# Two-sided decayed sums as a backward scan and a forward scan of it, in place, with clamps and one product on GpSimd

## The chip, the cores and the metric

The kernel runs on one core of a Trainium2 chip. A core has TensorE (PE, with its weight loads shown apart as PEld), VectorE (DVE), ScalarE (ACT), GpSimd (POOL) and SyncE (SP), and 16 DMA engines. The time is the device time of one launch in microseconds. Before the change it was 1601.48 us, the median of three runs (1598.72 to 1601.71).

## The reference, cut to what matters

Two layers, each a gated mixture of experts added to x. The gate comes from a conditioning signal that is computed from k = v = fside (4 batches, 512 steps, 512 channels) by a two-sided decayed sum over time. Here x is (4, 512, 512), everything is 32-bit floating point:

```python
def wkv(r, k, v, w, u, time_emb):            # r = x, k = v = fside
    tf    = sigmoid(sum(time_emb, -1))
    decay = exp(-exp(w)) * (0.5 + 0.5 * tf)  # one number for a batch and a channel
    ek, ekv = exp(min(k, 30)), exp(min(k, 30)) * v
    # a_t = decay * a_(t-1) + value_t, forward in time (nf, df) and backward (nb, db)
    euk = exp(min(u + k, 30))
    num = nf + nb - ekv + euk * v
    den = df + db - ek + euk
    return sigmoid(r) * (num / max(den, 1e-8)) * (0.8 + 0.2 * tf)

x = x + ffn0(wkv(x, fside, fside, w0, u0, cond), ...)   # rmsnorm, 8 routed experts, top 2, one shared
x = x + ffn1(wkv(x, fside, fside, w1, u1, cond), ...)   # 32 routed experts, top 6, capacity 512, shared
```

So num and den hold, for each step t, the sum over all steps s of decay^|t-s| times a value (ekv or ek), with one more term for t itself. Only the factor sigmoid(r) differs from layer to layer through x; the rest of layer 1's conditioning depends on fside alone.

## The kernel before

**The unit loop (layer 0's conditioning, L641 to L691).** Channels lie on the 128 partitions and time runs along the row. The work is cut into 16 units n = (b, c): batch b of 4, and one of four blocks of 128 channels; a unit is a tile of 128 x 512. The Python loop writes the order of the instructions on ACT, PE and DVE by hand (`tc.manual_schedule`, L193); POOL and SP are left to a planner, which places an instruction by the costs and the order that it assumes. In one pass of the loop stand, for different units:

- `turn(n + 3)`: PE transposes a block of k's rows (`kr`, one buffer, loaded by SP for a whole batch, L122) and ACT copies it to `kA` (L394, L395). After the last block of a batch the next batch's rows are asked for (L397), into the same buffer.
- `front(n + 1)`, `front_exps(n + 1)`: DVE clamps k and u + k at 30 (L406, L408), ACT takes both exponents (L414).
- `mid(n)`: DVE forms ekv and eukv (L425, L426) and runs four scans (`scans`, L263, L264): for den and for num a forward one, and a backward one of 511 columns that leaves the step itself out. Each writes a tile of its own.
- `sums(n - 1)`: PE adds the forward scan, the backward scan and the last term in PSUM, three pairs of matmuls for den and three for num (L436 to L438; the matrix for num carries the factor -(0.8 + 0.2 tf)). ACT then makes 1/den by logarithm and exponent (L440 to L442).
- `back(n - 1)`: DVE refines the reciprocal, multiplies by num and by sigmoid(x), four operations (L449 to L452). den has two banks of PSUM, num one.

Between these stand layer 0's routing for the batch before (`route_max`, `route_top`, `route_pay`, `route_slots`: some 45 small DVE instructions a batch, and eight indirect writes by POOL into a table in DRAM, L353) and the shared expert of a few token tiles. For batches 0 to 2 each table write waits for the one before it. Before the loop POOL writes the empty tables and fills the DRAM tensor `xb` with zeros, 16 writes of 256 KB (L245 to L254).

**The exponents of layer 1.** From unit 12 on, and in the shared expert's stretch after the loop, `exps1_upto` lets ACT take layer 1's exponents of units 0 to 9 into memory that has come free (`spare`); those of units 10 to 15 follow in `wkv1_rest`.

**Layer 0's routed experts and layer 1's conditioning (L904 to L954).** `routed(0, ...)` goes through 8 experts in tiles of 128 tokens: POOL gathers rows (L772), PE multiplies, ACT evicts, POOL forms `hrow` (L846) and scatters the result (L818). Here POOL, PE and ACT are in the written order and DVE is not: DVE's instructions are placed by the planner. DVE's work in this stretch is `wkv1(n)` for 16 units: clamp (L915), ekv (L916), the four scans, two adds of forward and backward (L918, L919), the terms of the step itself (L920 to L922), a floor (L923), a reciprocal (L924), and the product that replaces k in `kA` (L925). Its tiles are in the pool `rp`. After the last expert come the shared expert's last three token tiles (13, 14, 15; `LATE` is 13): `share_up` on PE (L580), `share_silu` on ACT (L585), `share_hid` on DVE (L591), then `share_turn` and `share_down`.

**The join (L957 to L987).** For each of 16 token tiles, the late ones first, SP loads the two halves of layer 0's result (`acc` from `xa`, L965, and `other` from `xb`, L967; the tiles of `other` are taken where the pool `rp` was), DVE adds them (L968, and L970 for the late tiles), PE transposes, ACT takes the sigmoid, and DVE multiplies by `kA` (L976) to make layer 1's input. Layer 1's shared and routed experts follow and take the rest of the time.

Of the kernel before, what the change touches and what calls it, by code (L numbers as in the profile page):

```python
# [9 lines left out]
F32 = mybir.dt.float32  # L10
# [3 lines left out]
ALU = mybir.AluOpType  # L14
# [11 lines left out]
DEN_MIN = 1e-8  # L26
EXP_LN = "natural_log_exp_and_others"
# [3 lines left out]
def adaln_ffn_kernel(  # L31
# [90 lines left out]
    def load_k(b):  # L122
        kr = wk.tile([P, TB, D], F32, tag="kr", name=f"kr{b}", bufs=1)
        nc.sync.dma_start(kr, kf[b * S : (b + 1) * S, :].rearrange("(i p) c -> p i c", p=P))
        return kr
# [54 lines left out]
    kr = wk.tile([P, TB, D], F32, tag="kr", name="kr0", bufs=1)  # L180
    for i in range(TB):
        nc.scalar.dma_start(kr[:, i, :], kf[i * P : (i + 1) * P, :])
    load_x(0)
    gaten = acc[:E1, NT - 3, :]
# [9 lines left out]
            engines={mybir.EngineType.Activation, mybir.EngineType.PE, mybir.EngineType.DVE}  # L194
# [20 lines left out]
    for l in range(2):  # L215
        ew = const.tile([P, NC], F32, name=f"ew{l}")
        nc.scalar.activation(ew, wch[l], AF.Exp)
        dw = const.tile([P, NC], F32, name=f"dw{l}")
        nc.scalar.activation(dw, ew, AF.Exp, scale=-1.0)
        dec = const.tile([P, NC, B], F32, name=f"dec{l}")  # L220
        nc.vector.tensor_tensor(
            dec, dw.unsqueeze(2).to_broadcast([P, NC, B]), half.unsqueeze(1).to_broadcast([P, NC, B]), ALU.mult
        )
        decay.append(dec)
# [20 lines left out]
    for tb, width in ((table0, 3), (table1, 2)):  # L245
        blank = wk.tile([P, NCOL * width], F32, name=f"blank{width}", tag="lgT", bufs=1)
        bv = blank.rearrange("p (c w) -> p c w", w=width)
        nc.gpsimd.memset(bv, 0.0)
        nc.gpsimd.memset(bv[:, :, 0], EMPTY)
        nc.gpsimd.dma_start(tb.rearrange("(p c) w -> p (c w)", p=P), blank)  # L250
    zero = wk.tile([P, D], F32, name="zero", tag="zr", bufs=TB)
    nc.gpsimd.memset(zero, 0.0)
    for t in range(NT):
        nc.gpsimd.dma_start(xb[t * P : (t + 1) * P, :], zero)  # L254


    L = S - 1

    def scans(l, b, c, ek, ekv, df, dx, nf, nx):

        dec = decay[l][:, c, b : b + 1]
        for v, f, r in ((ek, df, dx), (ekv, nf, nx)):
            nc.vector.tensor_tensor_scan(f, dec.to_broadcast([P, S]), v, 0.0, ALU.mult, ALU.add)  # L263
            nc.vector.tensor_tensor_scan(  # L264
                r[:, L - 1 :: -1],
                v[:, L:0:-1],
                dec.to_broadcast([P, L]),
                0.0,
                ALU.add,
                ALU.mult,  # L270
            )

# [113 lines left out]
    def turn(n):  # L386

        nonlocal kr
        if n >= NU:
            return  # L390
        b, c = units[n]
        pk = bank("tr", f"pk{n}")
        for i in range(TB):
            nc.tensor.transpose(pk[:, i * P : (i + 1) * P], kr[:, i, c * P : (c + 1) * P], ident)  # L394
        nc.scalar.copy(kA[:, c, b * S : (b + 1) * S], pk)  # L395
        if c == NC - 1 and b + 1 < NB:
            kr = load_k(b + 1)  # L397
            load_x(b + 1)

    def front(n):  # L400
        if n >= NU:
            return
        b, c = units[n]
        kT = kA[:, c, b * S : (b + 1) * S]
        ek = wk.tile([P, S], F32, tag="ek", name=f"ek{n}", bufs=2)
        nc.vector.tensor_scalar(ek, kT, 30.0, None, ALU.min)  # L406
        euk = wk.tile([P, S], F32, tag="euk", name=f"euk{n}", bufs=3)
        nc.vector.tensor_scalar(euk, kT, uch[0][:, c : c + 1], 30.0, ALU.add, ALU.min)  # L408
        fronts[n] = ek, euk

    def front_exps(n):
        if n < NU:
            for v in fronts[n]:
                nc.scalar.activation(v, v, AF.Exp)  # L414

    def mid(n):
        b, c = units[n]
        kT = kA[:, c, b * S : (b + 1) * S]
        ek, euk = fronts.pop(n)

        def tmp(tag, bufs=2):
            return wk.tile([P, S], F32, tag=tag, name=f"{tag}{n}", bufs=bufs)

        ekv, eukv = tmp("ekv", 1), tmp("eukv")
        nc.vector.tensor_tensor(ekv, ek, kT, ALU.mult)  # L425
        nc.vector.tensor_tensor(eukv, euk, kT, ALU.mult)  # L426
        df, dx, nf, nx = tmp("df"), tmp("dx"), tmp("nf"), tmp("nx")
        scans(0, b, c, ek, ekv, df, dx, nf, nx)
        mids[n] = (df, dx, euk), (nf, nx, eukv)

    def sums(n):

        b, c = units[n]
        den, num = bank("den", f"den{n}"), bank("num", f"num{n}")
        for p, m, (f, r, o) in zip((den, num), (ident, nfac[:, b, :]), mids.pop(n)):
            nc.tensor.matmul(p, m, f, start=True, stop=False)  # L436
            nc.tensor.matmul(p[:, :L], m, r[:, :L], start=False, stop=False)
            nc.tensor.matmul(p, m, o, start=False, stop=True)  # L438
        r = wk.tile([P, S], F32, tag="r", name=f"r{n}")
        nc.scalar.activation(r, den, AF.Relu, bias=neg_min)  # L440
        nc.scalar.activation(r, r, AF.Ln, bias=pos_min)
        nc.scalar.activation(r, r, AF.Exp, scale=-1.0)  # L442
        mids[n] = den, num, r
# [118 lines left out]
    def route_slots(b):  # L562
# [4 lines left out]
        through(fill_table(table0, sloti, pay, TB, 2, "table0" if b == NB - 1 else None))  # L567
# [53 lines left out]
    def exps1_upto(m):  # L621
        nonlocal done
        while done < m:
# [3 lines left out]
            nc.scalar.activation(ek, kT, AF.Exp)  # L627
# [13 lines left out]
    for n in range(NU + 1):  # L641
        b, c = divmod(n, NC)
        if n:
            sums(n - 1)
        front(n + 1)
# [29 lines left out]
        if c == 3 and b >= 1:  # L675
            route_slots(b - 1)
        if c == 2 and b >= 1:
            route_max(b - 1)
# [33 lines left out]
    route_slots(NB - 1)  # L712
    counts0 = const.tile([P, E0], I32, name="counts0")
# [190 lines left out]
    with tc.tile_pool(name="r0", bufs=1) as rp, tc.tile_pool(name="px0", bufs=1, space=PSUM) as px:  # L904
# [5 lines left out]
        def wkv1(n):  # L910
# [3 lines left out]
            ekv, df, dx, nf, nx = [rp.tile([P, S], F32, tag=f"v{i}", name=f"v{i}_{n}") for i in range(5)]  # L914
            nc.vector.tensor_scalar(ek, ek, E30, None, ALU.min)  # L915
            nc.vector.tensor_tensor(ekv, ek, kT, ALU.mult)  # L916
            scans(1, b, c, ek, ekv, df, dx, nf, nx)
            nc.vector.tensor_tensor(df[:, :L], df[:, :L], dx[:, :L], ALU.add)  # L918
            nc.vector.tensor_tensor(nf[:, :L], nf[:, :L], nx[:, :L], ALU.add)  # L919
            nc.vector.scalar_tensor_tensor(df, euk, E30, df, ALU.min, ALU.add)  # L920
            nc.vector.scalar_tensor_tensor(ekv, euk, E30, kT, ALU.min, ALU.mult)
            nc.vector.tensor_tensor(nf, nf, ekv, ALU.add)  # L922
            nc.vector.tensor_scalar(df, df, DEN_MIN, None, ALU.max)  # L923
            nc.vector.reciprocal(df, df)  # L924
            nc.vector.scalar_tensor_tensor(kT, nf, fac[:, b : b + 1], df, ALU.mult, ALU.mult)  # L925
# [188 lines left out]
```

## Time and profile before

| stretch of the span, us | what runs | PE busy | DVE busy | ACT busy | POOL busy |
|---|---|---|---|---|---|
| 60 to 120 | unit loop | 50.8 | 55.9 | 36.6 | 8.5 |
| 120 to 180 | unit loop with routing | 55.4 | 51.6 | 34.1 | 11.5 |
| 213 to 262 | shared expert, table, first gather | 45.4 | 18.6 | 22.7 | 14.7 |
| 262 to 395 | routed experts 0, `wkv1` on DVE | 112.9 | 133.0 | 61.0 | 89.9 |
| 395 to 468 | the same | 56.4 | 73.0 | 26.7 | 45.5 |
| 468 to 562 | routed experts 0 | 75.0 | 0.0 | 33.4 | 38.5 |
| 580 to 625 | join | 37.4 | 22.5 | 19.0 | 0.0 |

The profiled execution took 1601.9 us, its span (first to last instruction) is 1600.1 us at a mean granted PE clock of 0.963. Over the span PE is busy for 91%, DVE for 42%, POOL for 37% and ACT for 25%. Busy times are sums of instructions in the stretch; POOL's include the issue of its DMAs. In the listings a row gives its start, its duration, the engine, the line and the operation, and in brackets how long the engine had been idle before it and what ended that. Instructions of one engine overlap a little, so the distance from one start to the next is shorter than a duration.

### The profile page before, as it was taken

To read this page: it belongs to the slowest core of one execution; us is meant where nothing else is said; L and a number is where in the kernel's file an instruction comes from. 1 tells how busy PE (TensorE), PEld (TensorE's weight loads), DVE (VectorE), ACT (ScalarE), POOL (GpSimd) and SP (SyncE) were. 2 spreads that over 40 slices of the span, in tenths; PEclk is the share of its full clock that TensorE was granted. 3 is DMA by queue.
4 is the path that set the end of the run, shared out by engine and by line. 5 is a ranking of instruction groups with operands and counts; after the bars stand their busy time and mean duration, and the time that the engine had idled before them with its cause. 6 is when DMAs were issued, how large, how long until landed. Compare 5 with 4: busy or idle time off the path is not lost. (4 is left out here: it accounts for less than half of the span.)

```text
span 1600.1 us, 16354 instructions
## 1 busy us (share of the span) xinstructions
PE 1458.0 (91%) x5097; PEld 860.8 (54%) x5097; DVE 678.1 (42%) x1192; ACT 399.9 (25%) x966; POOL 593.0 (37%) x576
## 2 busy tenths in 40 slices
PE   4878988979788788999999999999999999999997
PEld 2445555656555466444444565555555555655654
DVE  6897956999960035261111222222222222222221
ACT  4755534454333324000000111111111111111110
POOL 3020133767654300016663333344333443433332
PEclk8999999999989879999999999999999999999999
DMA  9210114444545364001113655565645585565542
GB/s 351 80 33 34 40 47 163 73 100 77 111 109 125 86 223 153 1 1 43 39 46 109 181 150 130 145 191 153 164 109 136 128 266 119 130 187 131 122 99 40
DMA packets 117177, 184.95 MB, mean 116 GB/s; under 512 B 19928, under 2 KB 65004, under 8 KB 117016
## 3 DMA queue, kind: packets, MB, share of 16 engines
q1 hardware_dynamic: 80120, 122.14, 22.6%
q0 software_dynamic: 36336, 60.04, 19.8%
q8 instruction: 66, 1.08, 0.3%
q10 hardware_dynamic: 576, 1.05, 0.2%
q14 instruction: 79, 0.65, 0.1%
HBM read 152.07 MB, written 52.64 MB: 128 GB/s over the span
## 5 line engine op out<-in xcount | busy, mean ns | idle before, releaser
L813 PE MATMUL pout<-w,hT 128*128 128x512 f32 (+1 forms) x432 | 206.9, 612 | 10.6 <-ACT hT L804 9.3
L818 POOL DMA_INDIRECT out_dram<-ob,put x52 | 82.6, 1589 | 282.7 <-DVE ob L817 142.2
L772 POOL DMA_INDIRECT acc<-z1d,put x119 | 123.3, 1036 | 136.7 <-PE pza L785 58.9
L353 POOL DMA_INDIRECT table<-pay,r1sloti x96 | 93.3, 972 | 195.1 <-DVE hid L1063 168.6
L851 DVE SCALAR_TENSOR_TENSOR hrow<-pup,tab,sgt 128x352 f32<-128x352 f32 x84 | 49.1, 584 | 257.6 <-issue 131.2
L835 PE MATMUL pgate<-w,zgT 128*128 128x352 f32 x416 | 133.2, 463 | 0.1
L839 PE MATMUL pup<-w,zgT 128*128 128x352 f32 x416 | 131.5, 459 | 0.0
L817 DVE COPY ob<-pout 128x512 f32<-128x512 f32 x84 | 58.1, 692 | 172.7 <-PE pout L813 166.8
L813 PEld LDWEIGHTS pout<-w,hT 128*128 128x128 f32 (+1 forms) x432 | 77.8, 194 | 83.8 <-issue 55.7
L785 PE MATMUL pza<-ident,acc 128*128 128x128 f32 x584 | 88.8, 277 | 21.3 <-DMA acc<-z0d,put 18.1
L785 PEld LDWEIGHTS pza<-ident,acc 128*128 128x128 f32 x584 | 71.7, 142 | 65.3 <-issue 27.5
L353 POOL DMA_INDIRECT table<-r0pay,r0sloti x32 | 36.0, 1125 | 182.9 <-DVE r0sloti L343 137.4
L839 PEld LDWEIGHTS pup<-w,zgT 128*128 128x128 f32 x416 | 79.0, 190 | 44.0
L835 PEld LDWEIGHTS pgate<-w,zgT 128*128 128x128 f32 x416 | 75.8, 192 | 34.0 <-issue 1.2
L808 ACT COPY hT<-phT 96x128 f32<-96x128 f32 x84 | 22.0, 262 | 285.3 <-DVE hT L806 285.3
L1060 PE MATMUL g<-zT,w 128*128 128x512 f32 (+1 forms) x192 | 89.3, 609 | 4.2 <-DVE lg L991 4.2
L795 ACT COPY zgT<-pza 128x256 f32<-128x256 f32 x103 | 38.3, 373 | 210.3 <-DVE zgT L794 158.7
L813 PE MATMUL pout<-zT,hT 128*128 128x512 f32 (+1 forms) x192 | 87.8, 593 | 0.0
L1060 PE MATMUL u<-zT,w 128*128 128x512 f32 (+1 forms) x192 | 86.3, 592 | 0.0
L1069 PE MATMUL o<-w,hid 128*128 128x512 f32 (+1 forms) x192 | 83.8, 592 | 0.0
L835 PE MATMUL pgate<-zT,zgT 128*128 128x352 f32 x256 | 81.0, 459 | 0.0
L839 PE MATMUL pup<-zT,zgT 128*128 128x352 f32 x256 | 81.0, 459 | 0.0
(279 smaller groups left out, 2346.9 us busy)
## 6 DMA issues: line engine op xcount, KB each, us to landing
w<-in_L_ffn_w_dram SPq DMA_DIRECT2D x44, 704.0 KB, 5.9
zT<-in_L_ffn_w_dram SPq DMA_DIRECT2D x20, 704.0 KB, 5.0
w<-in_L_ffn_w_dram SPq DMA_DIRECT2D x22, 512.0 KB
zT<-in_L_ffn_w_dram SPq DMA_DIRECT2D x10, 512.0 KB
w<-in_L_ffn_w_dram SPq DMA_DIRECT2D x22, 192.0 KB, 8.9
xb<-zero POOLq DMA_DIRECT2D x16, 256.0 KB, 7.8
acc<-in_x_dram SPq DMA_DIRECT2D x4, 1024.0 KB, 15.2
z0d<-zr SPq DMA_DIRECT2D x16, 256.0 KB, 2.0
```

The lines of the kernel that those rows point to most:

```text
L353: ins = nc.gpsimd.indirect_dma_start(out=table, out_offset=bass.IndirectOffsetOnAxis(ap=sloti[:, t, j : j + 1], axis=0), in_=pay[:, t, j, ...
L772: nc.gpsimd.indirect_dma_start(out=rows(e, s), out_offset=None, in_=zd, in_offset=bass.IndirectOffsetOnAxis(ap=put_at[:, e * NS + s : e * ...
L785: nc.tensor.transpose(pza[which][:, c * P : (c + 1) * P], rows(e, s)[:, c * P : (c + 1) * P], ident)
L795: nc.scalar.copy(dst[:, h:, :], pza[which][:, h * P :].rearrange("p (c t) -> p c t", c=h))
L813: nc.tensor.matmul(po, hT[:m, j, :], dv[:m, j, :], start=(j == 0), stop=(j == nf - 1))
L817: nc.vector.tensor_copy(row, po)
L818: nc.gpsimd.indirect_dma_start(out=outs[n % len(outs)], out_offset=bass.IndirectOffsetOnAxis(ap=at, axis=0), in_=row, in_offset=None, boun ...
L835: nc.tensor.matmul(pg, zt[:, c, :], gv[:, c, :], start=(c == 0), stop=(c == NC - 1))
L839: nc.tensor.matmul(pu, zt[:, c, :], uv[:, c, :], start=(c == 0), stop=(c == NC - 1))
L851: nc.vector.scalar_tensor_tensor(hrow, pu, tab[:, col, 1:2], sgt, ALU.mult, ALU.mult)
L1060: nc.tensor.matmul(p[:m], wv[:, c, f : f + m], zT[:, c, cols], start=(c == 0), stop=(c == NC - 1))
L1069: nc.tensor.matmul(po, hid[:m, j, i * P : (i + 1) * P], dv[:m, j, :], start=(j == 0), stop=(j == len(FCH) - 1))
```

## The change

A backward scan over all 512 steps, followed by a forward scan of its result, gives at each step the two-sided sum divided by 1 - decay^2, up to the first step, where the backward result has to be multiplied by 1/(1 - decay^2) before the forward scan starts. So `scans` now works in place on one tile of two halves (den's and num's values): two backward scans, one scaling of the first column of both halves, two forward scans. The factor 1 - decay^2 enters as a bias (its logarithm) of the exponent in layer 0, and of layer 1's exponent too, whose clamp is now at 30's exponent times that factor (`cap`). For this each layer gets six more small DVE instructions and one ACT logarithm at the start.

In layer 0 the sums on PE fall from three pairs of matmuls to two each for den and num. The two clamps and the product eukv move from DVE to POOL. POOL joins the engines in the written order; its zero writes to `xb` are spread over the loop (one a pass), the empty tables are written in the pass n = 2, and the table writes of batches 0 to 2 are spread over three passes and no longer wait for each other. k's rows have two buffers, and the rows of batch 1 are asked for at the start, ahead of the gate's and the first experts' weights.

In layer 1 `wkv1` loses the two adds, keeps its clamp (now into the tile `v2`, no longer in place) and the rest.

```diff
-        kr = wk.tile([P, TB, D], F32, tag="kr", name=f"kr{b}", bufs=1)
+        kr = wk.tile([P, TB, D], F32, tag="kr", name=f"kr{b}")
...
     load_x(0)
+    krs.append(load_k(1))
...
-            engines={mybir.EngineType.Activation, mybir.EngineType.PE, mybir.EngineType.DVE}
+            engines={
+                mybir.EngineType.Activation, mybir.EngineType.PE, mybir.EngineType.DVE, mybir.EngineType.Pool
+            }
...
-        decay.append(dec)
+        nc.vector.tensor_scalar(dec, dec, NEAR_1, None, ALU.min)
+        om = const.tile([P, NC, B], F32, name=f"om{l}")
+        nc.vector.tensor_scalar(om, dec, -1.0, 1.0, ALU.mult, ALU.add)
+        nc.vector.scalar_tensor_tensor(om, dec, 1.0, om, ALU.add, ALU.mult)
+        lom = const.tile([P, NC, B], F32, name=f"lom{l}")
+        nc.scalar.activation(lom, om, AF.Ln)
+        inv = const.tile([P, NC, B], F32, name=f"inv{l}")
+        nc.vector.reciprocal(inv, om)
+        cap = const.tile([P, NC, B], F32, name=f"cap{l}")
+        nc.vector.tensor_scalar(cap, om, E30, None, ALU.mult)
+        decay.append((dec, cap, lom, inv))
...
-    def scans(l, b, c, ek, ekv, df, dx, nf, nx):
-
-        dec = decay[l][:, c, b : b + 1]
-        for v, f, r in ((ek, df, dx), (ekv, nf, nx)):
-            nc.vector.tensor_tensor_scan(f, dec.to_broadcast([P, S]), v, 0.0, ALU.mult, ALU.add)
+    def scans(l, b, c, v):
+
+        dec, _, _, inv = (m[:, c, b : b + 1] for m in decay[l])
+        for h in range(2):
             nc.vector.tensor_tensor_scan(
-                r[:, L - 1 :: -1],
-                v[:, L:0:-1],
-                dec.to_broadcast([P, L]),
-                0.0,
-                ALU.add,
-                ALU.mult,
+                v[:, h, ::-1], dec.to_broadcast([P, S]), v[:, h, ::-1], 0.0, ALU.mult, ALU.add
             )
+        nc.vector.tensor_scalar(v[:, :, 0], v[:, :, 0], inv, None, ALU.mult)
+        for h in range(2):
+            nc.vector.tensor_tensor_scan(v[:, h, :], dec.to_broadcast([P, S]), v[:, h, :], 0.0, ALU.mult, ALU.add)
...
-        nc.vector.tensor_scalar(ek, kT, 30.0, None, ALU.min)
+        v = wk.tile([P, 2, S], F32, tag="v2", name=f"v2_{n}", bufs=3)
+        nc.gpsimd.tensor_scalar(v[:, 0, :], kT, 30.0, None, ALU.min)
...
-        nc.vector.tensor_scalar(euk, kT, uch[0][:, c : c + 1], 30.0, ALU.add, ALU.min)
+        nc.gpsimd.tensor_scalar(euk, kT, uch[0][:, c : c + 1], 30.0, ALU.add, ALU.min)
...
-        nc.vector.tensor_tensor(ekv, ek, kT, ALU.mult)
-        nc.vector.tensor_tensor(eukv, euk, kT, ALU.mult)
+        nc.gpsimd.tensor_tensor(eukv, euk, kT, ALU.mult)
+        nc.vector.tensor_tensor(v[:, 1, :], v[:, 0, :], kT, ALU.mult)
+        scans(0, b, c, v)
...
-        for p, m, (f, r, o) in zip((den, num), (ident, nfac[:, b, :]), mids.pop(n)):
-            nc.tensor.matmul(p, m, f, start=True, stop=False)
-            nc.tensor.matmul(p[:, :L], m, r[:, :L], start=False, stop=False)
+        for p, m, (d, o) in zip((den, num), (ident, nfac[:, b, :]), mids.pop(n)):
+            nc.tensor.matmul(p, m, d, start=True, stop=False)
             nc.tensor.matmul(p, m, o, start=False, stop=True)
...
-        through(fill_table(table0, sloti, pay, TB, 2, "table0" if b == NB - 1 else None))
+        writes[b] = fill_table(table0, sloti, pay, TB, 2, "table0")
...
             sums(n - 1)
+            nc.gpsimd.dma_start(xb[(n - 1) * P : n * P, :], zero)
+        if n == 2:
+            blank_tables()
...
             route_slots(b - 1)
+            write_slots(b - 1, 3)
+        if c < 2 and b >= 2:
+            write_slots(b - 2, 3 - c if b < NB else 5)
...
-            ekv, df, dx, nf, nx = [rp.tile([P, S], F32, tag=f"v{i}", name=f"v{i}_{n}") for i in range(5)]
-            nc.vector.tensor_scalar(ek, ek, E30, None, ALU.min)
-            nc.vector.tensor_tensor(ekv, ek, kT, ALU.mult)
-            scans(1, b, c, ek, ekv, df, dx, nf, nx)
-            nc.vector.tensor_tensor(df[:, :L], df[:, :L], dx[:, :L], ALU.add)
-            nc.vector.tensor_tensor(nf[:, :L], nf[:, :L], nx[:, :L], ALU.add)
+            v = rp.tile([P, 2, S], F32, tag="v2", name=f"v2_{n}", bufs=1)
+            cap = decay[1][1][:, c, b : b + 1]
+            nc.vector.tensor_scalar(v[:, 0, :], ek, cap, None, ALU.min)
+            nc.vector.tensor_tensor(v[:, 1, :], v[:, 0, :], kT, ALU.mult)
+            scans(1, b, c, v)
+            d, s = v[:, 0, :], v[:, 1, :]
...
```

## The prediction

> **What bounds the kernel now.** I read the table of stages first (busy microseconds of each engine in stretches that I chose), then the waits, then the VectorE (DVE) timeline around the places that the diff touches. The page's own chain of waits covers 2% of the span and carries nothing. Columns: PE, PEld, DVE, ACT and POOL busy, then the granted clock and the DMA.
>
> ```profile
> 120.00:180.00 60.00, 55.42 (x193) 31.05 (x192) 51.55 (x113) 34.14 (x62) 11.50 (x10) 0.94 0.14 50
> ...
> 213.00:262.00 49.00, 45.40 (x184) 31.07 (x183) 18.56 (x72) 22.70 (x45) 14.73 (x16) 0.97 0.19 65
> 262.00:395.00 133.00, 112.93 (x465) 79.34 (x465) 132.99 (x137) 60.96 (x178) 89.88 (x56) 0.95 0.48 108
> 395.00:468.00 73.00, 56.42 (x223) 38.77 (x221) 73.00 (x77) 26.70 (x87) 45.45 (x32) 0.92 0.47 109
> 468.00:562.00 94.00, 75.04 (x273) 51.54 (x274) 0.00 (x1) 33.40 (x105) 38.49 (x34) 0.86 0.45 103
> ```
>
> Layer 0's unit loop (to 213) is DVE's: one unit follows the next at 9.24 us (46.35 to 55.59) and its DVE instructions fill that. From 213 to 262 PE runs the shared expert. From 262 to 557 PE runs the routed experts of layer 0, while DVE works through layer 1's conditioning (`wkv1`), done at 468. DVE's next work is the last three token tiles of the shared expert and then the join of the layers:
>
> ```profile
> 464.66 3.34 DVE L924 RECIPROCAL v<-v 128x512 f32<-128x512 f32 x1
> 562.54 0.48 DVE L591 SCALAR_TENSOR_TENSOR shr<-pza,rs,ssg 128x256 f32<-128x256 f32 x1 [94.54 <-ACT ssg L585]
> 562.95 0.74 DVE L925 SCALAR_TENSOR_TENSOR kA<-v,fac,v 128x512 f32<-128x512 f32 x1
> 566.00 0.48 DVE L591 SCALAR_TENSOR_TENSOR shr<-pza,rs,ssg 128x256 f32<-128x256 f32 x1 [2.31 <-ACT ssg L585]
> 572.26 0.48 DVE L591 SCALAR_TENSOR_TENSOR shr<-pza,rs,ssg 128x256 f32<-128x256 f32 x1 [5.78 <-ACT ssg L585]
> 580.38 0.69 DVE L968 TENSOR_TENSOR acc<-acc,other 128x512 f32<-128x512 f32 x1 [7.64 <-DMA other<-xb]
> ```
>
> The reader is to see the 94.54 us wait: DVE stands at the first L591 until PE has left the routed experts. It costs nothing, because only one instruction of `wkv1` (L925 of unit 15) is queued behind it before the join.
>
> **Part 1, the order on DVE (decides).** While `routed(0)` is built, DVE is not under the written order; the planner places its instructions. In the changed program as built, the three `share_hid` (now L606) stand here:
>
> ```
> unit 10: L938 L939 L278x2 L281 L283x2 L942 | L606 tile 13 | L943 L945 L944 L946 | L606 tile 14 | L947
> unit 11: L938 L939 L278x2 L281 | L606 tile 15 | L283x2 L942 L943 L945 L944 L946 L947
> units 12 to 15, then the first add of the join (L990)
> ```
>
> DVE runs its queue in order, so the rest of unit 10 and units 11 to 15 now wait for PE to finish the routed experts, and the join needs them: its gate (L998) multiplies by `kA`, late tiles first, which are units 12 to 15, and its first add stands behind them on DVE. What each costs, by start to start distances in the rows of before: reciprocal 3.27, scan 1.13, two-input operation 0.60, one-input 0.34, L925 0.74, and 0.1 more where an instruction reads the one before it. A unit of before takes 12.27 (L916 at 273.41 and 285.68). The change drops two adds (0.58 + 0.60), brings L938's clamp into the unit (0.40; nine of the 16 had been done before 262) and adds the two-column scaling between the scans (0.3 with its dependencies): 12.0. From 562.54: tile 13's product 0.41, L943 to L946 5.0, second product 0.4 (its input is there at 566.0), L947 0.7, unit 11 to its scaling 3.5, third product (input at 572.2, DVE there at 572.6) 0.4, rest of unit 11 8.5, making 581.5; four units 48.0, making 629.5. The loads of `other` lie in memory that the pool of `wkv1` gives back (their first waits for DVE among others), so 3.0 us from issue to first add as now (577.38 to 580.38): 632.5 against 580.38, **+52**. Bounds: +49 if the loads are early, +54 if the second product also holds up PE. The 45 us of the join itself stay: PE starts it after an idle stretch now too, at a clock of 0.50 in 580 to 600.
>
> **Part 2, the unit loop.** Rows:
>
> ```profile
> L263 DVE TENSOR_TENSOR_SCAN df<-dec,ek 128x512 f32<-128x512 f32 x16 | 19.5, 1217 | 0.0
> ...
> L426 DVE TENSOR_TENSOR eukv<-euk,kA 128x512 f32<-128x512 f32 x16 | 10.9, 684 | 0.0
> ...
> L408 DVE TENSOR_SCALAR euk<-kA,chan 128x512 f32<-128x512 f32 x16 | 7.7, 482 | 0.0
> L406 DVE TENSOR_SCALAR ek<-kA 128x512 f32<-128x512 f32 x16 | 6.8, 423 | 0.3 <-ACT kA L395 0.3
> ```
>
> Four scans stay four scans, of 512 instead of 511 columns. DVE loses two clamps and a product, 0.33 + 0.40 + 0.60 by distance, and gains the scaling, 0.3 (nearest row: 128x4 operations, 0.17): -1.03 a unit, -16.5 for 16. Five clamps of layer 1 (L915) that now sit between 160 and 213 leave it: -1.7. Two matmul pairs a unit go from PE (0.86 each by distance); only the last unit's are on the path: -1.7. The second buffer of k's rows removes this wait:
>
> ```profile
> PE pk L394 <- DMA kr<-in_fside_BxSxS_dram: 11.7, 4, 8.0
> ```
>
> which reached DVE as 6.87 at 36.6 and 0.86 before it: -7.7. The load of rows 1 passes the gate, router and expert weights on SP's queue; the 16 zero writes (0.55 us each on POOL, 4 MB) leave the first 23 us, so I take those loads as no later. The start gains two round trips DVE to ACT to DVE for the logarithm before the first copies (11.31 now): +2.4. Small waits of DVE on ACT and PE between 122 and 212 sum to 9.5; with PE lighter I take -4 (0 to -9.5).
>
> POOL gets two one-input and one two-input 512-column operations a unit. Only `hrow` (256 columns, 722 ns alone) shows what that costs DVE:
>
> ```profile
> 390.35 0.95 POOL L846 TENSOR_TENSOR hrow<-upt,sgt 128x256 f32<-128x256 f32 x1 [1.81 <-ACT upt L845]
> ```
>
> ```profile
> 390.69 1.69 DVE L264 TENSOR_TENSOR_SCAN v<-spare,dec 128x511 f32<-128x511 f32 x1
> ```
>
> The scan took 1.69 instead of 1.20. Over the 26 `hrow` from 262 to 468 DVE lost 8.3 us: 0.5 where it met a scan, 0.32 on average. Doubled to 512 columns the product holds DVE for 1.0; a clamp I set at 0.45, the memset's slope (515 - 205 ns over 384 columns) times 512. A unit's three come just after the sums of two units ago, which is during its scans, so I take 80% of 1.92 for 15 units: +23 (ends: 0.32 each, +14; all of it for 16 units, +31). Loop: -16.5 - 1.7 - 1.7 - 7.7 + 2.4 - 4 + 23 = **-6** (-21 to +7).
> The Trainium skill, "SBUF — State Buffer", section "Who interferes with whom", says that a DVE instruction with two SBUF inputs contends with a GpSimd instruction that reads SBUF, and that the first holds the pair for the whole instruction. By it the hold would be the whole 1.24 + 2 x 0.65, +38, and the time 1659; the row's 0.49 of 0.72 us is what I go by.
>
> POOL's queue: in units with table writes, three (0.97 each, 1.9 when DVE is busy) stand before the next clamps. Those have about 15 us until their scan, so they are covered; uncovered, a unit would slip by some 4. The 24 early writes no longer wait for each other (35.8 us of POOL idle, off the path: the last eight come at 231.8 as before), 0. ACT's exponent with a column as bias costs 0.1 more (718 against 636), hidden in ACT's 26 idle us of 60.
>
> **Part 3, the routed experts.** DVE reaches the wait near 395 instead of 468. In 285 to 460 PE waited 10.0 us for gathered rows, in 475 to 565 0.9; 73 more quiet us and fewer two-input operations give **-4** (0 to -10).
>
> **Sum.** 52 - 6 - 4 = +42 on the profiled execution: span 1600.1 to 1642, its time 1601.9 to 1644. It lies 0.4 above the median 1601.48, so 1643.5.
>
> **Rivals.** (a) Slower than I say: POOL holds DVE for all of its time (+31 instead of +23, which is 8 more), the small waits stay (4), the quiet stretch gives nothing (4) and the join starts at +54 (2): 1656 to 1662 for most or all of these. For it: POOL's own `hrow` took 3.04 to 3.45 us where it met runs of two-input operations. Against: the 0.32 on average. (b) Less slow: the loop gains its -21 and the experts -10: 1619 to 1626. (c) Faster: the first L606 does not hold `wkv1`, so the +52 is not paid: 1591. It decides if fewer than a unit (12 us less the gains of 10) stands behind the wait. Only a tile 13 ready by 395 does that, and PE makes it after the last expert, at 557 now. (d) The change does nothing for the loop, POOL giving back exactly what DVE lost: Part 1 alone, 1650, inside the range.
>
> **Chances.** Forecast, with (d), 1626 to 1656: 0.80; (a) 0.08; (b) 0.08; (c) 0.04. The range is that of the first. A measurement of this kernel tells about 0.2% (3.2 us) from no change. (c) is all of faster but for a sliver at no change; the rest is slower.
>
> **What would show it.** DVE idle from about 390 to 555 before L606 of tile 13; 67 us of DVE work between that and the first L990, PE nearly idle in the last 50; `wkv1` units at 12.0; the loop's units near 9.8 where no routing stands, with scans of 1.6 and more beside POOL's operations; no PE wait for `kr` after 12. Wrong: a join that starts within 15 us of the third product, or a loop end beyond 225.

## The result, and the profile after

The changed kernel takes 1656.01 us (median of 4 runs, 1653.19 to 1666.63) against 1601.60 of the kernel before beside it: 1.0356 times, 95% interval 1.0308 to 1.0404. Forecast were 1643.5 us and a range of 1626 to 1656. The direction and the place were right. The forecast was 12.5 us too low, and the time lies just past the upper end of the range. The profiled execution took 1653.2 us, with a span of 1651.2.

The stages of the changed kernel, in the stretches that were shown of before (PE, PEld, DVE, ACT and POOL busy, granted clock, DMA share, GB/s):

```profile
120.00:180.00 60.00, 48.95 (x157) 26.87 (x158) 42.86 (x90) 30.05 (x54) 32.70 (x25) 0.81 0.14 53
...
262.00:395.00 133.00, 111.08 (x453) 77.64 (x452) 125.92 (x131) 64.11 (x177) 70.43 (x53) 0.95 0.47 109
395.00:468.00 73.00, 60.39 (x246) 42.28 (x245) 11.85 (x12) 28.34 (x93) 36.94 (x33) 0.95 0.44 98
468.00:562.00 94.00, 74.50 (x292) 51.89 (x292) 2.55 (x5) 35.03 (x109) 40.29 (x36) 0.93 0.51 119
562.00:580.00 18.00, 10.42 (x36) 5.90 (x34) 17.69 (x20) 1.85 (x5) 0.00 (x0) 0.91 0.64 231
580.00:625.00 45.00, 0.00 (x0) 0.00 (x0) 44.16 (x49) 0.00 (x0) 0.00 (x0) 0.50 0.00 0
```

The last line is the change in one row: from 580 to 625, where the kernel before ran the join, PE, ACT and the DMAs do nothing and DVE works alone. The VectorE timeline of the changed kernel says on what:

```profile
406.46 0.67 DVE L942 SCALAR_TENSOR_TENSOR v<-spare,v 128x512 f32<-128x512 f32 x1
559.45 0.48 DVE L606 SCALAR_TENSOR_TENSOR shr<-pza,rs,ssg 128x256 f32<-128x256 f32 x1 [152.32 <-ACT ssg L600]
559.85 0.68 DVE L943 SCALAR_TENSOR_TENSOR spare<-spare,kA 128x512 f32<-128x512 f32 x1
...
564.65 0.39 DVE L606 SCALAR_TENSOR_TENSOR shr<-pza,rs,ssg 128x256 f32<-128x256 f32 x1
...
569.49 0.48 DVE L606 SCALAR_TENSOR_TENSOR shr<-pza,rs,ssg 128x256 f32<-128x256 f32 x1
...
628.00 0.75 DVE L947 SCALAR_TENSOR_TENSOR kA<-v,fac 128x512 f32<-128x512 f32 x1
632.06 0.69 DVE L990 TENSOR_TENSOR acc<-acc,other 128x512 f32<-128x512 f32 x1 [3.31 <-DMA other<-xb]
```

DVE stops in the middle of unit 10 (L942), waits 152.32 us for the shared expert's tile 13, and only then does the rest of unit 10 and units 11 to 15. The join's first add comes 72.61 us after the first of the three products; in the kernel before it was 17.84. So the time went as follows (us against the profile of before; the last column is a second profile of the same kernel, run e9_after_again):

| stretch | forecast | after | second profile |
|---|---|---|---|
| to the second gather of the routed experts (262.44 before) | -6 | +6.7 | +6.6 |
| second gather to the first L606 (300.1 before) | -4 | -9.8 | -3.4 |
| first L606 to the join's first add (17.84 before) | +52 | +54.8 | +54.7 |
| join, layer 1, to the end (1019.7 before) | 0 | -0.6 | -2.6 |
| sum | +42 | +51.1 | +55.3 |

Two questions are left for the experiments: is it the order on DVE alone that makes the late join, and why did the stretch with the unit loop get longer by some 7 us where it should have got shorter by 6?

### The profile page after: what moved, and what is told of

Same layout as the page of the kernel before. It is cut to its first block, busy times and chain, and to the rows that moved or that the text cites. A ratio compares the mean times of both kernels' runs of the same rounds, so it can differ in the third digit from the quotient of the medians.

```text
span 1651.2 us, 16246 instructions
## 1 busy us (share of the span) xinstructions
PE 1436.1 (87%) x5033; PEld 849.3 (51%) x5033; DVE 674.6 (41%) x1154; ACT 404.2 (24%) x968; POOL 658.4 (40%) x624
## 5 line engine op out<-in xcount | busy, mean ns | idle before, releaser
L835 PEld LDWEIGHTS pout<-w,hT 128*128 128x128 f32 (+1 forms) x432 | 77.2, 193 | 86.6 <-issue 54.7
L283 DVE TENSOR_TENSOR_SCAN v<-dec,v 128x512 f32<-128x512 f32 x64 | 79.9, 1291 | 1.1
```

The lines of the kernel that those rows point to most:

```text
L283: nc.vector.tensor_tensor_scan(v[:, h, :], dec.to_broadcast([P, S]), v[:, h, :], 0.0, ALU.mult, ALU.add)
L835: nc.tensor.matmul(po, hT[:m, j, :], dv[:m, j, :], start=(j == 0), stop=(j == nf - 1))
```

## The experiments

All of them start from the changed kernel. "Loop" is the distance from the first product v by kA to that of unit 15: 183.05 us before, 190.07 in the changed kernel.

### The order on DVE: e1_order and e10_two_v

```diff
-        with tc.manual_schedule(engines={mybir.EngineType.Pool, mybir.EngineType.PE, mybir.EngineType.Activation}):
+        with tc.manual_schedule(
+            engines={mybir.EngineType.Pool, mybir.EngineType.PE, mybir.EngineType.Activation, mybir.EngineType.DVE}
+        ):
```

> The changed kernel with VectorE in the written order through the routed experts of layer 0, so that the shared expert's last three products stand behind all 16 units of layer 1's conditioning, as before the change. Nothing else differs. Theory (the order decides): the join's first add comes about 18 us after the first of the three products, as before (17.8), not 72.6 us after it; the first product comes at 560 to 569 (VectorE is busy to about 470 again, so up to 9.8 us that the routed experts had gained go back). Time 1656 - 55 + (0 to 10) = 1601 to 1611, within 0.6% of the kernel before. Rival (the join is late for another reason, the loads of the second half or the memory they wait for): the first add still comes more than 40 us after the first product, and the time stays above 1630.

Measured: 1602.74 us (10 runs), 1.0011 of before, interval 0.9991 to 1.0031. The VectorE timeline of this run:

```profile
566.04 0.48 DVE L606 SCALAR_TENSOR_TENSOR shr<-pza,rs,ssg 128x256 f32<-128x256 f32 x1 [84.32 <-ACT ssg L600]
569.50 0.48 DVE L606 SCALAR_TENSOR_TENSOR shr<-pza,rs,ssg 128x256 f32<-128x256 f32 x1 [2.97 <-ACT ssg L600]
575.76 0.48 DVE L606 SCALAR_TENSOR_TENSOR shr<-pza,rs,ssg 128x256 f32<-128x256 f32 x1 [5.78 <-ACT ssg L600]
583.91 0.69 DVE L992 TENSOR_TENSOR acc<-acc,other 128x512 f32<-128x512 f32 x1 [7.66 <-DMA other<-xb]
```

The wait of 84 us is still there, but nothing of `wkv1` is queued behind it, and the first add (L992 in this file) comes 17.87 us after the first product. The order carries the whole late join, and 53 us of the 54 that the change costs.

What made the planner put the products there? The tile of `wkv1` has one buffer in the changed code, so one unit cannot begin before the last has ended. The next run changes only that, and leaves DVE to the planner.

```diff
-            v = rp.tile([P, 2, S], F32, tag="v2", name=f"v2_{n}", bufs=1)
+            v = rp.tile([P, 2, S], F32, tag="v2", name=f"v2_{n}", bufs=2)
```

> The changed kernel with two buffers instead of one for the tile of layer 1's conditioning; VectorE's order is left to the planner. As built, the planner then overlaps the units (the reciprocal of one unit is followed by a scan of the next) and puts the first of the three products behind the scaling of unit 15 instead of into unit 10; 9.4 us of unit 15 stand between it and the third. Theory (the one buffer stretches the planned units and so moves the products forward): the first product waits for TensorE as before, its third comes about 10 us later as before, the join's first add about 18 us after the first product; time 1598 to 1606, as with VectorE in the written order. A unit of layer 1 falls from 13.3 us to about 12.7 while the routed experts run. Rival (TensorE's products or the loads keep the join late): the first add more than 25 us after the first product, time above 1612.

Measured: 1605.22 us (10 runs), 1.0025, interval 1.0007 to 1.0043; the first ten units of layer 1 are 11.94 us apart on average (13.12 in the changed kernel, 12.73 before). Its VectorE timeline:

```profile
567.91 0.48 DVE L606 SCALAR_TENSOR_TENSOR shr<-pza,rs,ssg 128x256 f32<-128x256 f32 x1 [116.75 <-ACT ssg L600]
568.31 2.33 DVE L283 TENSOR_TENSOR_SCAN v<-dec,v 128x512 f32<-128x512 f32 x2
...
571.36 0.48 DVE L606 SCALAR_TENSOR_TENSOR shr<-pza,rs,ssg 128x256 f32<-128x256 f32 x1
...
573.30 3.35 DVE L946 RECIPROCAL v<-v 128x512 f32<-128x512 f32 x1
...
577.63 0.48 DVE L606 SCALAR_TENSOR_TENSOR shr<-pza,rs,ssg 128x256 f32<-128x256 f32 x1 [0.19 <-ACT ssg L600]
585.96 0.69 DVE L990 TENSOR_TENSOR acc<-acc,other 128x512 f32<-128x512 f32 x1 [7.85 <-DMA other<-xb]
```

The products now stand in unit 15, whose remaining 9.1 us fit between the first product and the third; the first add comes 18.05 us after the first product. One buffer more, 4 KB a partition, is worth 51 us, though the work that it speeds up is off the path in either kernel. That the single buffer is what moved the products is shown; how the planner weighs them was not looked into.

### POOL's arithmetic in the loop: e2_dve and e5_dve_again

With the written order of e1_order, clamps and product go back to DVE:

```diff
-        nc.gpsimd.tensor_scalar(v[:, 0, :], kT, 30.0, None, ALU.min)
+        nc.vector.tensor_scalar(v[:, 0, :], kT, 30.0, None, ALU.min)
...
-        nc.gpsimd.tensor_scalar(euk, kT, uch[0][:, c : c + 1], 30.0, ALU.add, ALU.min)
+        nc.vector.tensor_scalar(euk, kT, uch[0][:, c : c + 1], 30.0, ALU.add, ALU.min)
...
-        nc.gpsimd.tensor_tensor(eukv, euk, kT, ALU.mult)
+        nc.vector.tensor_tensor(eukv, euk, kT, ALU.mult)
```

> The run with the mended order, and besides it both clamps and the product euk times k of layer 0 on VectorE again; POOL keeps only its DMAs in the loop. Theory (POOL's arithmetic costs the loop more than it takes from VectorE): the loop, from the first product of unit 0 to that of unit 15, goes from 190 to about 179 us (183 before, less the 7.7 us wait for k's rows, plus 15 scalings of 0.26), so about 11 us less time than with the mended order alone. Rival (POOL's arithmetic is worth having and the loop is long for another reason, the chain of in-place scans or the late x): the loop gets longer by up to 21 us, which is 16 times 1.33 us of VectorE work.

> The mended order with clamps and product on VectorE once more, in more rounds, beside the next two on the same chip. Expected: 0.995 of the kernel before with an interval below 1, as in the first run of it.

Measured: 1594.48 us, 0.9954 (0.9932 to 0.9977), loop 176.76; the same kernel again 1592.97 us, 0.9943 (0.9924 to 0.9963), loop 175.20. With the arithmetic on POOL (e1_order) the loop was 189.87: POOL costs it 13 to 15 us (11 were expected), though it takes 21.3 us of work (16 times 1.33, by distance) from DVE. The groups of the loop on DVE (busy us, mean ns of one, idle us before them), first e1_order, with POOL's arithmetic:

```profile
L278 DVE TENSOR_TENSOR_SCAN v<-dec,v 128x512 f32<-128x512 f32 x30 | 38.7, 1331 | 0.5
...
L436 DVE TENSOR_TENSOR v<-v,kA 128x512 f32<-128x512 f32 x16 | 13.0, 814 | 1.6 <-ACT v L427 1.6
...
L281 DVE TENSOR_SCALAR v<-v,inv 128x2 f32<-128x2 f32 x15 | 7.8, 520 | 0.5
```

then e2_dve, without:

```profile
L278 DVE TENSOR_TENSOR_SCAN v<-dec,v 128x512 f32<-128x512 f32 x32 | 37.4, 1211 | 0.6
...
L436 DVE TENSOR_TENSOR v<-v,kA 128x512 f32<-128x512 f32 x16 | 10.9, 682 | 0.0
...
L281 DVE TENSOR_SCALAR v<-v,inv 128x2 f32<-128x2 f32 x16 | 3.7, 229 | 0.6
```

Two costs show. DVE's instructions are longer beside POOL's: mean differences times counts are 3.6 (L278), 2.2 (L283), 2.1 (L436), 1.9 (L458), 1.3 (L460) and 4.3 us (L281), and 2.4 for small instructions of the routing, together 17.8. And DVE stands idle longer, 9.6 us of it in one wait.

The loop can be added up on DVE without a rest: it is the duration of DVE's instructions, plus the idle time between them (here every gap, the shortest too), less the time that neighbours overlap. Against e2_dve, this run and those of the next two sections differ so (us, rounded; the work that moved is at the durations of e2_dve):

| run | work moved to POOL | other instructions longer | idle time | less overlap | loop |
|---|---|---|---|---|---|
| e1_order | -22.8 | +17.8 | +14.4 | +3.8 | +13.1 |
| e3_early | -22.8 | +27.3 | -2.2 | +3.3 | +5.7 |
| e4_prod | -10.2 | +16.2 | -2.6 | +1.1 | +4.5 |
| e7_clamps | -12.5 | +8.5 | +0.4 | +2.3 | -1.3 |

### Where the waits come from: e3_early

The timeline of the changed kernel from 109 to 131, all engines, with the lines that follow from one another:

```profile
109.12 1.35 POOL L365 DMA_INDIRECT table<-r0pay,r0sloti  x1 [0.16 <-issue]
110.78 1.12 POOL L365 DMA_INDIRECT table<-r0pay,r0sloti  x1 [0.31 <-issue]
112.20 1.48 POOL L365 DMA_INDIRECT table<-r0pay,r0sloti  x1 [0.30 <-issue]
113.67 0.61 POOL L660 DMA_DIRECT2D xb<-zero  x1
114.36 2.47 POOL L418 TENSOR_SCALAR v<-kA 128x512 f32<-128x512 f32 x1
116.86 0.72 ACT L427 ACTIVATE v<-v,lom 128x512 f32<-128x512 f32 x1 [6.10 <-POOL v L418]
...
119.50 0.63 ACT L615 COPY shT<-sph 128x256 f32<-128x256 f32 x2
...
119.91 1.12 PE L405 MATMUL pk<-ident,kr 128*128 128x128 f32 x4 [7.12 <-ACT shT L615]
...
130.44 0.17 DVE L509 TENSOR_SCALAR v<-ssq 128x4 f32<-128x4 f32 x1 [9.62 <-ACT sq L479]
```

Three table writes and a zero write stand before the clamp on POOL. The scan that uses the clamp's result comes much later, but ACT stops at its exponent (6.10 us), and behind that exponent in ACT's order is the copy of the shared expert's rows (L615); PE waits for that copy (7.12) with the routing's transposes queued behind; DVE waits for their squares (9.62). To test it, the clamps go one pass earlier, ahead of the writes:

```diff
     front(0)
+    front(1)
     front_exps(0)
...
-        front(n + 1)
         front_exps(n + 1)
...
             mid(n)
+            front(n + 2)
```

> The run with the mended order, and besides it POOL's two clamps one pass earlier: they stand in POOL's queue ahead of the table writes of the pass before, POOL does the same work. Theory 1 (late clamps: the table writes stand ahead of them on POOL, ScalarE waits in order for the clamp, then PE for ScalarE, then VectorE): the 9.6 us wait of VectorE for the squares at 130 goes and ScalarE's 19.1 us of waits for POOL's first clamp fall below 5; the loop shortens by 8 to 12 us. Theory 2 (the shared port alone): VectorE's scans stay as long as they are (1.28 to 1.33 us on average) and the loop changes by less than 3 us.

Measured: 1598.22 us, 0.9971 (0.9951 to 0.9990), loop 182.42, which is 7.5 shorter than with the late clamps. DVE's waits in the loop fall from 20.8 to 4.2 us, and the 9.6 is gone. These are all that are left (us in total, times, longest):

```profile
DVE t L457 <- ACT r L450: 2.2, 1, 2.2
DVE v L436 <- ACT v L427: 1.6, 1, 1.6
DVE r0sm L303 <- ACT r0pr L300: 0.4, 1, 0.4
```

ACT's waits before its exponent of the clamp (L427) fall from 20.3 to 1.2 us. That is theory 1, with 7.5 us just short of its 8 to 12. The idle time on DVE falls by 16.6 us, but more than half of that comes back, which neither theory had: DVE's instructions get longer beside POOL's. The group of the backward scans is now

```profile
L278 DVE TENSOR_TENSOR_SCAN v<-dec,v 128x512 f32<-128x512 f32 x32 | 46.9, 1506 | 0.6
```

and the lengthening over e2_dve is 27.3 us instead of 17.8 (L278 9.4 instead of 3.6). If each DVE instruction is put to the POOL operation that it lies beside longest, the product's share goes from 10.1 to 19.1 us, and that of the clamps stays (7.4 and 8.1).

### The product alone and the clamps alone: e4_prod and e7_clamps

Both with the written order. The first has only the product on POOL; the second only the clamps, one pass early as in e3_early.

> The run with the mended order, and besides it the two clamps on VectorE again; only the product euk times k stays on POOL. Against the run with all three on VectorE, VectorE loses 16 times 0.60 us (9.6) and meets one POOL operation a unit instead of three. If the port costs what that operation takes alone (1.27 us a unit, 20 us), the loop is up to 11 us longer than with all on VectorE; if it costs 0.3 us a unit, about 5 us shorter. From the lengthening of VectorE's instructions in the changed kernel (about 15 us for 48 POOL operations) I expect 5 us shorter.

> The mended order, the product euk times k on VectorE, both clamps on POOL and one pass early, ahead of the table writes. VectorE loses 16 times 0.73 us (11.7) against all three on VectorE. The product alone on POOL cost VectorE 14 us (181.2 - 176.8 + 9.6); all three together lengthened VectorE's instructions by 15.4 us. Theory (a two-input operation on POOL holds up VectorE, a one-input one hardly does): the loop is 168 to 171 us and this is the fastest kernel so far. Rival (any POOL operation costs VectorE about half of its own time; the two clamps take 1.5 and 2.0 us each alone or nearly so): the loop is 16 times 1.75 us longer less 11.7, about 193 us, or no shorter than 176 if only a third of that holds.

The product alone: loop 181.23, so 4.5 longer than with all on DVE (176.76) although DVE has 9.6 us less to do; the 5 us gain that was expected did not come. The groups of this run:

```profile
L278 DVE TENSOR_TENSOR_SCAN v<-dec,v 128x512 f32<-128x512 f32 x32 | 46.5, 1494 | 0.6
...
L436 DVE TENSOR_TENSOR v<-v,kA 128x512 f32<-128x512 f32 x16 | 13.2, 824 | 0.1
...
L281 DVE TENSOR_SCALAR v<-v,inv 128x2 f32<-128x2 f32 x16 | 5.5, 346 | 0.6
```

Over the loop L278 is longer by 9.1 us in all, L436 by 2.3, L458 by 1.9, L281 by 1.9 and L283 by 1.0: 16.2 us for 16 products, 1.0 for one that takes 1.26 us undisturbed. The time was 1607.01 us, 1.0001 (0.9970 to 1.0031); its seven runs lie between 1595.7 and 1610.8, more apart than the loop explains. In its profile the join and layer 1 alone took 1026.3 us, against 1016.8 in that of e2_dve.

The clamps alone: loop 175.41, level with all on DVE (176.76 and 175.20); 1593.06 us, 0.9927 (0.9897 to 0.9956). Here too the hoped-for gain did not come, nor the rival's loss. The groups of this run:

```profile
L278 DVE TENSOR_TENSOR_SCAN v<-dec,v 128x512 f32<-128x512 f32 x32 | 41.2, 1329 | 0.6
...
L281 DVE TENSOR_SCALAR v<-v,inv 128x2 f32<-128x2 f32 x16 | 6.4, 397 | 0.6
```

DVE's instructions are longer by 8.5 us (L278 3.8, L281 2.7, the rest in small parts), 0.26 for each clamp; with more idle time and less overlap that uses up what DVE was spared. So the two-input product on POOL costs DVE about four times as much as a one-input clamp, though the clamps take longer themselves (1.49 and 2.00 us). It is not that the clamps happen to lie where DVE does little: they lie beside its scans for 38.7 us here and make them 4.2 longer, the products of e4_prod for 17.2 us and make them 10.1 longer.

### The second buffer of k's rows: e6_one_kr and e8_zero_first

To price the second buffer of k's rows, it is taken away from e5_dve_again, and the rows are loaded as before:

```diff
-        kr = wk.tile([P, TB, D], F32, tag="kr", name=f"kr{b}")
+        kr = wk.tile([P, TB, D], F32, tag="kr", name=f"kr{b}", bufs=1)
...
-    krs.append(load_k(1))
...
+            krs.append(load_k(b + 1))
             load_x(b + 1)
-            if b + 2 < NB:
-                krs.append(load_k(b + 2))
```

> The mended order with clamps and product on VectorE, and besides it one buffer for k's rows again, loaded where the kernel before loads it. Theory (the wait for k's rows is 7.7 us of the loop's 6.3 us gain over the kernel before): the loop goes from 176.8 to 183 to 185 us, TensorE waits for k's rows for some 8 us again, and the time is level with the kernel before (0.998 to 1.002). Rival (the wait is hidden once VectorE has less to do, or the in-place scans bring the gain): the loop stays below 179 us.

The next run takes the spread of the zero writes away as well: all 16 before the loop, none in it.

> The run with one buffer for k's rows, and besides it the 16 zero writes (4 MB) at the start again, where the kernel before has them. There the wait of TensorE for k's rows was 3.7 us and cost VectorE nothing (loop 175.2); rows 1 were asked for at 17.1 instead of 22.3. Theory (the zero writes in the first 23 us keep the other loads back; spreading them is what took the wait away, not the second buffer): rows 1 are asked for near 22 and land near 35 again, TensorE waits for them for 7 to 9 us, VectorE for 6 to 7, and the loop is 181 to 183 us. Rival (the lighter VectorE and TensorE work is what brings the request forward): request near 17, wait below 4 us, loop below 177 us.

Measured: with one buffer 1595.84 us, 0.9955 (0.9934 to 0.9976), loop 175.18: no loss. With the zero writes early too, 1595.81 us, 0.9959 (0.9935 to 0.9983), loop 176.04. The waits of PE, first with one buffer,

```profile
PE pk L404 <- DMA kr<-in_fside_BxSxS_dram: 3.7, 1, 3.7
```

then with the zero writes early too,

```profile
PE pk L406 <- DMA kr<-in_fside_BxSxS_dram: 8.3, 1, 8.3
```

and one row of the VectorE timeline, of the kernel before and of that last run:

```profile
43.49 0.69 DVE L449 SCALAR_TENSOR_TENSOR t<-den,r 128x512 f32<-128x512 f32 x1 [6.87 <-ACT r L442]
...
41.46 0.69 DVE L457 SCALAR_TENSOR_TENSOR t<-den,r 128x512 f32<-128x512 f32 x1 [1.04 <-ACT r L450]
```

The zero writes do hold k's rows back (asked for at 23.6 us instead of 17.1, and PE waits 8.3 instead of 3.7): that part of the theory stands. But the whole wait of the kernel before, 8 us on PE, now costs DVE 1.04 instead of 6.87. 2.0 of the 5.8 are won by PE, which ends den's sums behind the wait at 39.3 instead of 41.3 (a pair of matmuls fewer); 3.8 are not won but come from DVE, which started the loop that much later (18.02 against 14.26) and comes to them at 40.4 instead of 36.6. Of the 7.7 us that I gave the buffer, a second buffer and spread writes together bring 1.7 at the most (the product of unit 15 at 192.39 and at 194.06), and that is no more than two profiles of one kernel differ: in e2_dve, the same kernel as e5_dve_again, it came at 193.84. With the arithmetic on POOL this was not tried.

### Again, and the two repairs together: e9_after_again and e11_two_v_dve

> The changed kernel again, unaltered, for a second profile. In eight profiles in which VectorE works through layer 1's conditioning without the wait, the stretch from the second gather to the first of the three products took 294.1 to 303.7 us (mean 298.8); in the profile of the changed kernel 290.3. Theory (the routed experts run faster while VectorE stands still): below 293 us again. Rival (chance): within 294 to 304. The time is expected at 1650 to 1660.

Measured: 1655.35 us, 1.0335 (1.0312 to 1.0358). The stretch from the second gather to the first L606 took 296.7 us, not below 293: the theory's own bound is missed. Eleven profiles without the early wait, the kernel before among them, lie between 294.1 and 303.7 (mean 298.9), the two of the changed kernel at 290.3 and 296.7. A gain of the routed experts from a quiet DVE may be there, but profiles that differ by 9 us among themselves cannot price it; it stays open.

The last run joins the two repairs, two buffers in `wkv1` with the planner's order, and clamps and product on DVE:

> The same with clamps and the product of layer 0 on VectorE. Expected: what the mended order gave with these on VectorE, 0.994 of the kernel before (1590 to 1596 us); if the overlapped units disturb POOL's products in the routed experts more, up to 5 us longer.

Measured: 1592.14 us, 0.9949 (0.9930 to 0.9968), loop 176.72, the join's first add 17.91 us after the first product. It is faster than both kernels: some 8 us, which is what the rest of the change is worth without the late join and without arithmetic on POOL. Which of its parts (in-place scans, lighter sums, order of the loads) brings it was not taken apart. It does not differ from e5_dve_again, e7_clamps or e6_one_kr by more than their intervals.

## Why the prediction was right and where it was wrong

By its parts the profile missed the forecast by +2.8 (late join), +12.7 (loop), -5.8 (quiet stretch) and -0.6 (the rest): 9 us. The other 3 of the 12.5 are in the median, which lies 2.8 above the profiled execution, where that of the kernel before lay 0.4 below.

**Part 1, the late join: right in mechanism, place and size.** The rest of unit 10 and units 11 to 15 stood behind the wait; the first add came at 632.06 where 632.5 was worked out. Taken from the first product it is +54.8 instead of +52: the units took 12.56 us, not 12.0. That term was mis-sized because the new unit is one chain. The timeline shows 0.72 us from L939's start to that of the scan that reads it, where before independent neighbours stood 0.58 to 0.60 apart, and 3.38 instead of 3.27 for the reciprocal. Two adds saved 1.18, the clamp cost 0.52 instead of 0.40, the scaling 0.27, and the dependencies the rest. e1_order and e10_two_v show that no other cause is needed.

**Part 2, the loop: this is the step that failed.** Forecast -6, measured +6.7. The range (-21 to +7) just held it, but the ends that were named for it add up to +5.8. Added up on DVE as in the experiments, with gaps of more than 0.1 us as waits:

| term, us | forecast | measured |
|---|---|---|
| DVE's own work, and what lies before and after the loop | -16.5 - 1.7 - 1.7 + 2.4 = -17.5 | -12.5 |
| POOL's hold on DVE (its instructions longer beside POOL's) | +23 | +17.8 |
| waits of DVE in the loop (rows of k, small waits) | -7.7 - 4 = -11.7 | +1.4 |

- *The waits, and with them "Those have about 15 us until their scan, so they are covered":* the failed sentence. 11.7 us of waits were to go, and 1.4 came (20.9 against 19.5): 13.1 worse, as much as the whole miss of this stretch; the other two terms cancel. It asked when the clamp's data is needed, and not who waits for it first: ACT, in order, with the shared expert's copy and the routing's squares behind it. And it took a clamp at 0.65 us of POOL (in its +38); they take 1.49 and 2.00 at the least, so that clamps, product and zero write fill 6 to 7 us of POOL in a unit before any table write. With the clamps ahead of the writes (e3_early) the waits were 4.1 us, so the forecast gain was there to be had.
- *POOL's hold on DVE:* 5.2 better than forecast in the changed kernel, but 27.3 where POOL is not late. For the product the scaling from `hrow` was near: `hrow` cost a scan 0.49 of its 0.72 us, and alone on POOL (e4_prod) the product cost DVE the 1.0 that was set for it, of its 1.26. The clamps are cheaper (0.26 each, not 0.45; the memset's slope, by which that was set, gives 0.41). The Trainium skill's "SBUF — State Buffer", section "Who interferes with whom", calls the pair of ports that DVE shares with POOL an exclusive lock and says, of the 2-port modes, that the first to issue keeps it for the whole instruction. The mean in e4_prod is 80% of the product; single products v by kA went from 0.68 to 1.82 us, so in single cases the hold is nearly whole.
- *DVE's own work:* 5.0 worse. Some 3 of it is the in-place chain: in the old order an independent neighbour starts about 0.08 us before the one ahead of it ends; an instruction that reads the one ahead of it starts 0.03 after. Now the first scan reads the product, and the scaling separates scans that overlapped, which is 0.2 us a unit that I had not counted. The rest was not taken apart. (At the start stand five more small DVE instructions a layer, not the six named under the change.)
- *Rows of k, -7.7:* the wait is gone, but by e8_zero_first most of it was not to be had: there DVE lost 1.04 to it with one buffer and early writes.

**Part 3, the quiet stretch, -4:** -9.8 and -3.4 in the two profiles, inside 0 to -10, but not shown to be more than scatter. That the first was -9.8 is luck: it hid almost half of Part 2's miss, and in the second profile the parts add up to +55.3 where +42 was forecast.

**The rivals.** (a), 1656 to 1662, named the time but not quite the way: the small waits did stay and the join was at +54.8, but POOL held DVE for less than I forecast, not more, and the late clamps were not among its conditions. (b) fell with the loop. (c) fell: DVE stood at the first L606 for 152 us with five units behind it. (d), a loop that nets zero, was 7 us too kind.

**What was to be seen.** DVE idle from 407 to 559 (390 to 555 foretold), 69 us of its work before the join (67), PE idle in the last 50, scans of 1.6 beside POOL's operations, no wait for k's rows: all there. The loop's units near 9.8 were not: 33.23, 41.67, 52.60 and 63.53 are the products of units 2 to 5, 10.9 apart in the last two steps.

## What to carry to other kernels

Where a planner orders an in-order engine, read the order that came out, for a buffer count far from the path can move a long wait in front of work that is on it: here one buffer was worth 51 us. Of work moved to another engine, ask not only when its result is needed, but which in-order engine stops for it first and what is queued behind that instruction there. And price the moved operation by its own duration on the new engine plus what it takes from the old one: alone on POOL the product cost VectorE 1.0 us where it had cost 0.60.

## What the runs showed of the hardware that was not expected

- POOL's one-input clamps are slower than its two-input product. These three rows of the changed kernel follow each other:

```profile
123.74 1.50 POOL L418 TENSOR_SCALAR v<-kA 128x512 f32<-128x512 f32 x1
125.34 2.00 POOL L420 TENSOR_SCALAR euk<-kA,chan 128x512 f32<-128x512 f32 x1
127.43 1.27 POOL L435 TENSOR_TENSOR eukv<-euk,kA 128x512 f32<-128x512 f32 x1
```

  At the least the clamp takes 1.49 us, add and clamp 2.00, the product 1.25 (on DVE 0.42, 0.48, 0.68). The Trainium skill's "GPSIMD Engine Reference", section "4.1 Engine selection", calls one-input operations roughly line-rate; these rows say otherwise.
- The 128x2 scaling L281, 0.23 us alone, took up to 1.24 beside the product (e4_prod) and 0.52 on average in e1_order: a tiny DVE operation can wait for most of a POOL instruction.
- The price of one and the same POOL operation to DVE is not fixed. The 16 products lengthened DVE's instructions by 10.1 us in e1_order, 16.1 in e4_prod and 19.1 in e3_early, though they lay beside them for 23 to 26 us each time; the clamps cost 7.4 to 8.3 us in every run. What sets the product's price was not settled.
